# Graph attention on one core: from dense masked scores to a gathered list of edges

## The chip, the core and the metric

The kernel runs on one core of a Trainium2 chip. The metric is device time in microseconds (us). The kernel before took 4289.51 us, the median of 3 runs that lie between 4289.07 and 4289.96.

The engines are named as the profile names them: PE is TensorE (matrix products; PEld its weight loads), DVE is VectorE, ACT is ScalarE, POOL is GpSimd, and SP is SyncE, which here only starts transfers. SBUF is the on-chip memory of 128 partitions, PSUM holds the results of products, DRAM is the memory outside.

## The reference

There are 16 batches of 1024 nodes with 512 features, 8 heads of 64, and one 0/1 matrix `adj` of 1024 x 1024 for all batches. All is float32.

```python
q = (x @ Wq + bq).reshape(b, n, H, HD)          # k, v likewise
scores = einsum('bqhd,bkhd->bhqk', q, k) / sqrt(HD)
scores = scores + (1.0 - adj)[None, None, :, :] * -1e9
out = einsum('bhqk,bkhd->bqhd', softmax(scores, -1), v).reshape(b, n, d)
y = layernorm(x + out @ Wo + bo)
```

`adj` is sparse: entry (i, j) is 1 with probability 0.0039 times a weight that falls as one over the square root of i and of j. With the inputs given it has 4043 ones. The eight tiles of 128 rows have, counting a row without ones as one edge, 1404, 592, 446, 382, 368, 320, 301 and 290 edges, and the largest number in one row is 66, 10, 7, 9, 8, 6, 6 and 6. A row without ones gets the mean of all values, since its scores are all equally masked.

## The kernel before

All 1024 x 1024 scores of a head are computed, and a mask takes out those that aren't edges. `mask_setup` turns `adj` once into `maskT` (bf16, key by query: 0 or a large negative number). In `scores`, for a pair of heads, half of the queries (512) and a tile of 128 keys, PE makes two products with 64 rows (L325), DVE adds the mask while it takes the result out of PSUM (L329), ACT takes the exponential (L332), and POOL adds the result into a running sum over keys (L337, L339). `weigh` multiplies by the values (L347). `normalise` sums over partitions with a product with ones (L357), inverts (L359) and scales (L361).

While batch b runs, the pieces of `batch_work(b)` are put between: `finish` of batch b-1 (output projection L304, bias, residual, layer norm on DVE with a power on POOL, L301 to L316), the transposes of x for batch b+1 (L257) and its projections (`project_v` L266, `project_qk` L273). SP starts the loads of x and the stores of the result.

The tile framework orders the instructions of each engine when it builds the program, and puts in the waits; each engine then runs its list in order. So the order that a reader sees in the loops below isn't quite the order on an engine. Buffers are named by a tag and a number of copies (`bufs`); who asks for a copy waits until its last reader is done.

At the end a guard (`flag`) tests that the inputs are in the range that this method can do; if not, `tile_general` computes everything again in a general way.

Of the kernel before, what the change touches and what calls it, by code (L numbers as in the profile page):

```python
# [19 lines left out]
MASKED = -(2.0 ** 30)  # L20
LIMIT = (28.0 * 8.0) ** 2
# [101 lines left out]
def kernel(  # L123
# [25 lines left out]

    nc = tc.nc  # L150
# [4 lines left out]
    HALF = N // 2  # L155
    scale = 1.0 / HD ** 0.5
    assert N == 1024 and D == 512 and HD == 64

# [11 lines left out]

    with ExitStack() as main:
# [3 lines left out]
        psum = main.enter_context(tc.tile_pool(name="psum", bufs=1, space=bass.MemoryType.PSUM))  # L175

        def fill_psum(name):
            return psum.tile([P, HALF], F32, tag="fill", name=name, bufs=2)

        ones = one.tile([P, P], F32, name="ones")  # L180
        nc.gpsimd.memset(ones, 1.0)
        neg_half = one.tile([P, 1], F32, name="neg_half")
        nc.gpsimd.memset(neg_half, -0.5)

        pick = one.tile([P, 32], BF16, name="pick")
        nc.gpsimd.memset(pick, 0.0)
        nc.gpsimd.memset(pick[0:HD, 0:1], 1.0)
        nc.gpsimd.memset(pick[HD:P, 1:2], 1.0)
        gmax = one.tile([P, B * NPAIR], F32, name="gmax")
        maskT = one.tile([P, NT, N], BF16, name="maskT")  # L190
        nz_bc = one.tile([P, N], BF16, name="nz_bc")
        check = one.tile([P, NT], F32, name="check")

        XB, XT, V, QT, KT, OT, SQ = {}, {}, {}, {}, {}, {}, {}

        def load_x(b, t):

            if t < NT // 2:
                XB[b, t] = work.tile([P, 2, D], F32, tag="xb", name=f"xb_{b}_{t}", bufs=2)
                nc.sync.dma_start(XB[b, t], x[b, ds(t * 2 * P, 2 * P), :].rearrange("(j p) d -> p j d", p=P))  # L200
# [6 lines left out]
        nc.scalar.dma_start(bo_bc, bass.AP(tensor=bo.tensor, offset=bo.offset, ap=[[0, P], [1, D]]))  # L207

        def bias_setup():
# [7 lines left out]
            bvb = work.tile([P, NPAIR, P], F32, tag="y", name="bvb", bufs=2)  # L217
# [6 lines left out]
        def mask_setup(t):  # L224
            a = work.tile([P, N], F32, tag="prob", name=f"a_{t}", bufs=5)
            nc.sync.dma_start(a, adj[ds(t * P, P), :])
            j = work.tile([P, N], F32, tag="prob", name=f"a2_{t}", bufs=5)
# [14 lines left out]
            for k in range(NT):  # L242
                nc.tensor.transpose(pm[:, k // 4, ts(k % 4, P)], a[:, ts(k, P)], ident)  # L243
# [119 lines left out]
        def front_work(b):  # L363

            for t in range(NT):
                yield lambda t=t: project_v(b, t)
# [108 lines left out]
```

## Time and profile before

| what | value |
|---|---|
| median of 3 runs | 4289.51 us (4289.07 to 4289.96) |
| the profiled execution's own time | 4287.69 us |
| its span, first to last instruction | 4285.9 us |
| granted PE clock, mean | 0.992 |
| busy: PE, PEld, DVE, ACT, POOL | 4188.4, 1494.7, 2192.9, 1482.6, 2333.6 us |
| moved by DMA | 111.69 MB, mean 26 GB/s |

The span and the time of the same execution differ by 1.8 us. Busy time is the time in which at least one instruction of the engine ran; a product is shown longer than it holds PE, since products are pipelined. One float32 product is two rows of the trace on PE. A group's line names the source line, the engine, the operation, output and input, shapes, count, busy time and mean duration, and behind the second bar the idle time of that engine just before, with what ended it.

### The profile page before, as it was taken

The numbers are of one execution on the slowest core, as the hardware profiler recorded it, in microseconds if no ns is written. First come the engines' busy times: TensorE is split into PE (matmuls) and PEld (weight loads), VectorE is DVE, ScalarE is ACT, GpSimd is POOL, SyncE is SP. The second block draws the span as 40 slices with busy tenths as digits, with TensorE's granted clock in tenths as the row PEclk, the third lists the DMA queues.
The fourth block names the chain that finished last, engine by engine and source line by source line (L and its number), as shares of the span: only waits on it lengthen the run. The fifth ranks groups of instructions, "written<-read, shape, count | busy, mean of one in ns | idle before, by whom it ended". The sixth has DMA issues, their size and how long they took to land.

```text
span 4285.9 us, 35469 instructions
## 1 busy us (share of the span) xinstructions
PE 4188.4 (98%) x13660; PEld 1494.7 (35%) x13660; DVE 2192.9 (51%) x2200; ACT 1482.6 (35%) x1665; POOL 2333.6 (54%) x1163
## 2 busy tenths in 40 slices
PE   6999999999999999999999999999999999999987
PEld 3333333333333333333333333333333333333322
DVE  4345545454554544545455454545545445454565
ACT  1333333333333333333333333333333333333331
POOL 0355656555465555656555565554655556565575
PEclk8999999999999999999999999999999999999998
DMA  3000101010010100101000010100101001010001
GB/s 115 20 1 27 32 0 59 1 40 20 1 59 0 55 5 15 45 0 59 0 30 30 0 59 0 42 18 3 57 1 57 3 17 42 1 50 0 20 20 35
DMA packets 57882, 111.69 MB, mean 26 GB/s; under 512 B 5340, under 2 KB 5352, under 8 KB 57704
## 3 DMA queue, kind: packets, MB, share of 16 engines
q1 hardware_dynamic: 55424, 104.88, 7.7%
q10 hardware_dynamic: 2280, 4.46, 0.3%
q8 instruction: 109, 1.79, 0.2%
q14 instruction: 69, 0.57, 0.0%
HBM read 75.77 MB, written 33.55 MB: 26 GB/s over the span
## 4 chain that ended last, share of the span: by engine, by line
PE 92%; POOL 2%; DVE 2%; DMA 1%; issue 1%; ACT 0%; SPq 0%; POOLq 0%; DVEq 0%; ACTq 0%
PE sc L325 24%; PE av L347 21%; PE pv L266 11%; PE pq L273 11%; PE pk L273 11%; PE po L304 10%; PE den L357 3%; POOL acc L339 2%; PE pxT L257 2%; PE pg L294 1%; DMA y<-in_x_dram 1%; DVE rc L359 1%; DVE y L315 0%; DVE e L329 0%; DMA out_dram<-y 0%
## 5 line engine op out<-in xcount | busy, mean ns | idle before, releaser
L339 POOL TENSOR_TENSOR acc<-acc,e 128x1024 f32<-128x1024 f32 x768 | 1805.4, 2351 | 1113.1 <-ACT e L332 1081.8
L329 DVE TENSOR_TENSOR e<-sc,maskT 128x1024 f32<-128x1024 f32 x1024 | 1213.2, 1218 | 828.4 <-PE sc L325 828.0
L332 ACT ACTIVATE e<-e 128x1024 f32<-128x1024 f32 x1024 | 1082.5, 1057 | 1327.7 <-DVE e L329 1275.0
L325 PE MATMUL sc<-qT,kT 64*128 64x512 f32 x4096 | 1168.8, 622 | 12.8 <-DVE e L329 12.6
L347 PE MATMUL av<-e,v 128*64 128x512 f32 x4096 | 993.3, 606 | 0.0
L337 POOL TENSOR_TENSOR acc<-e,e 128x1024 f32<-128x1024 f32 x128 | 300.2, 2345 | 585.1 <-ACT e L332 585.0
L325 PEld LDWEIGHTS sc<-qT,kT 64*128 64x128 f32 x4096 | 385.0, 186 | 614.4 <-issue 505.7
L359 DVE RECIPROCAL rc<-den 128x512 f32<-128x512 f32 x128 | 429.5, 3355 | 145.8 <-PE den L357 145.8
L347 PEld LDWEIGHTS av<-e,v 128*64 128x64 f32 x4096 | 248.6, 136 | 683.4 <-issue 606.8
L304 PE MATMUL po<-wo,oT 128*128 128x512 f32 x1024 | 474.7, 607 | 3.0 <-DVE y L307 3.0
L266 PE MATMUL pv<-wv,xT 128*128 128x512 f32 x1024 | 472.7, 605 | 0.0
L273 PE MATMUL pq<-xT,wq 128*128 128x512 f32 x1024 | 472.5, 605 | 0.0
L273 PE MATMUL pk<-xT,wk 128*128 128x512 f32 x1024 | 472.2, 604 | 0.0
L304 PEld LDWEIGHTS po<-wo,oT 128*128 128x128 f32 x1024 | 185.0, 190 | 291.7 <-issue 271.9
L273 PEld LDWEIGHTS pq<-xT,wq 128*128 128x128 f32 x1024 | 184.4, 189 | 285.7 <-issue 285.7
L273 PEld LDWEIGHTS pk<-xT,wk 128*128 128x128 f32 x1024 | 184.6, 189 | 284.9 <-issue 284.9
L266 PEld LDWEIGHTS pv<-wv,xT 128*128 128x128 f32 x1024 | 184.8, 190 | 283.9 <-issue 248.2
L282 DVE SCALAR_TENSOR_TENSOR qT<-pq,bias_qk,nz_bc 128x512 f32<-128x512 f32 x128 | 96.1, 751 | 329.2 <-ACT sq L278 329.2
L295 DVE TENSOR_REDUCE gmax<-pg 128x1 f32<-128x512 f32 x64 | 44.3, 692 | 369.5 <-PE pg L294 369.5
L307 DVE TENSOR_TENSOR y<-po,y 128x512 f32<-128x512 f32 x128 | 88.1, 688 | 272.6 <-PE po L304 263.5
L278 ACT ACTIVATE sq<-pq,bias_qk 128x512 bf16<-128x512 f32 x128 | 87.9, 687 | 395.1 <-PE pq L273 395.1
L301 POOL TENSOR_TENSOR y<-y,bo_bc 128x512 f32<-128x512 f32 x128 | 163.0, 1273 | 108.9 <-PE pm L243 61.0
(65 smaller groups left out, 1201.1 us busy)
## 6 DMA issues: line engine op xcount, KB each, us to landing
xb<-in_x_dram SPq DMA_DIRECT2D x64, 512.0 KB, 3.7
y<-in_x_dram SPq DMA_DIRECT2D x128, 256.0 KB, 2.6
out_dram<-y SPq DMA_DIRECT2D x128, 256.0 KB, 2.1
a<-in_adj_dram SPq DMA_DIRECT2D x8, 512.0 KB, 4.5
wq<-in_L_gnn_Wq_dram ACTq DMA_DIRECT2D x1, 1024.0 KB, 9.0
wk<-in_L_gnn_Wk_dram ACTq DMA_DIRECT2D x1, 1024.0 KB
wv<-in_L_gnn_Wv_dram ACTq DMA_DIRECT2D x1, 1024.0 KB, 17.4
wo<-in_L_gnn_Wo_dram ACTq DMA_DIRECT2D x1, 1024.0 KB, 19.6
```

What stands on the lines that cost most here:

```text
L266: nc.tensor.matmul(p, XT[b][:, c, ts(t, P)], W["v"][:, c, :], start=(c == 0), stop=(c == NPAIR - 1))
L273: nc.tensor.matmul(p, W[name][:, c, ts(hp, P)], XT[b][:, c, ts(n, HALF)], start=(c == 0), stop=(c == NPAIR - 1))
L301: nc.gpsimd.tensor_tensor(y, y, bo_bc, op=OP.add)
L304: nc.tensor.matmul(p, OT[b, c, t // 4][:, ts(t % 4, P)], W["o"][:, c, :], start=(c == 0), stop=(c == NPAIR - 1))
L325: nc.tensor.matmul(sc[:, h, :], KT[b, hp][ts(h, HD), ts(kt, P)], QT[b, hp, n][ts(h, HD), :], start=True, stop=True)
L329: nc.vector.tensor_tensor(e, sc, maskT[:, kt, None, ts(n, HALF)].to_broadcast([P, 2, HALF]), op=OP.add)
L332: nc.scalar.activation(e, e, AF.Exp)
L337: nc.gpsimd.tensor_tensor(ACC[u], PR[b, hp, n, 0], e, op=OP.add)
L339: nc.gpsimd.tensor_tensor(ACC[u], ACC[u], e, op=OP.add)
L347: nc.tensor.matmul(AV[u][ts(h, HD), :], V[b, kt][:, ds(hp * P + h * HD, HD)], e[:, h, :], start=(kt == 0), stop=(kt == NT - 1),)
L357: nc.tensor.matmul(den[ts(h, HD), :], ones[:, 0:HD], acc[:, h, :], start=True, stop=True)
L359: nc.vector.reciprocal(rc, den)
```

## The change

The scores are computed for edges alone.

- **Edges (`edges`, once).** From `adj`, DVE takes the column numbers of the ones of each row out in order, 8 at a time (MAX, then a pass that sets those to zero): ten rounds for the first tile of 128 rows, two for the others. Each row gets a run of places in a list; blocks of 128 places are the unit of work. The eight tiles have 11, 6, 4, 4, 3, 3, 3 and 3 blocks (37 together). For each place the list holds the row of its key (`key_row`) and of its query (`query_row`); `sums` holds for each block a 128 x 128 0/1 matrix from places to queries.
- **Projections.** q, and k beside v, are computed per tile of 128 nodes with the nodes on partitions, and written to DRAM (`q_rows`, `kv_rows`; two copies each, by the batch's parity). The sums of squares for the guard are on ACT and DVE.
- **Per block (16 x 37 = 592).** `gather` starts two indirect transfers on POOL: 128 rows of k and v (4 KB each) and 128 rows of q (2 KB each). `scores` multiplies q and k on DVE and sums by head; ACT takes the exponential of 128 x 8 numbers. `weigh` multiplies the values by it on DVE. `add_up` sums over the edges of each query with two products with the 0/1 matrix. Masks, the large exponentials and POOL's running sums are gone.
- **Per tile of queries.** `normalise` divides, `transpose_o` transposes on PE for the output projection, `finish` is as it was.
- **Order.** `gather` runs 6 blocks ahead of `add_up`, `scores` 2 and `weigh` 1, as the loop is written. Each turn of the loop also takes one piece of the next batch's projections (24 per batch), or a `finish`.

The guard now also tests that each tile has no more edges than places, and no row more than 80 (first tile) or 16 ones.

The core of the diff (new text; what it replaces is named above):

```diff
-MASKED = -(2.0 ** 30)
-LIMIT = (28.0 * 8.0) ** 2
+LIMIT = 28.0 ** 2
+BLOCKS = (11, 6, 4, 4, 3, 3, 3, 3)
+DEGREE = (80, 16, 16, 16, 16, 16, 16, 16)
+KEYCODE = 2000.0
...
+        kv_rows = [dram.tile([N + 1, 2 * D], F32, name=f"kv_rows_{i}") for i in range(2)]
+        q_rows = [dram.tile([N, D], F32, name=f"q_rows_{i}") for i in range(2)]
...
+        def edges(t):
+            nb, J = BLOCKS[t], DEGREE[t]
+            a = work.tile([P, N], F32, tag="kvg", name=f"a_{t}", bufs=8)
             nc.sync.dma_start(a, adj[ds(t * P, P), :])
+            v = work.tile([P, N], F32, tag="kvg", name=f"codes_{t}", bufs=8)
+            nc.gpsimd.tensor_tensor(v, a, code, op=OP.mult)
...
+            for r in range(J // 8):
+                nc.vector.max(out=kl[:, ts(r, 8)], in_=v)
+                if r < J // 8 - 1:
+                    nc.vector.scalar_tensor_tensor(
+                        v, v, kl[:, r * 8 + 7:r * 8 + 8], v, op0=OP.is_lt, op1=OP.mult
+                    )
...
+            nc.vector.tensor_scalar(ge[:, 0:nb * P], span, kl[:, J:J + 1], None, op0=OP.is_ge)
+            nc.vector.scalar_tensor_tensor(of[:, 0:nb * P], span, end, ge[:, 0:nb * P], op0=OP.is_lt, op1=OP.mult)
...
+                for i in range(n):
+                    nc.tensor.matmul(g[:, i, :], of[:, ts(i0 + i, P)], kl, start=True, stop=True)
...
+        def norm(b, t, i, s):
...
+            nc.scalar.activation(sq, s, AF.Square)
+            nc.vector.tensor_reduce(
+                NRM[b][:, i, t, :], sq.rearrange("p (h d) -> p h d", d=HD), axis=AX.X, op=OP.add
+            )
+
+        def front_q(b, t):
+            p = project(b, t, "q")
+            q = work.tile([P, D], F32, tag="q", name=f"q_{b}_{t}", bufs=3)
+            nc.vector.scalar_tensor_tensor(q, p, scale, bq_bc, op0=OP.mult, op1=OP.add)
+            nc.sync.dma_start(q_rows[b % 2][ds(t * P, P), :], q)
+            norm(b, t, 0, q)
+
+        def front_k(b, t):
...
+            nc.vector.tensor_tensor(KV[b, t][:, 0:D], p, bk_bc, op=OP.add)
+            norm(b, t, 1, KV[b, t][:, 0:D])
+
+        def front_v(b, t):
...
+            nc.scalar.copy(kv[:, D:], p)
+            nc.sync.dma_start(kv_rows[b % 2][ds(t * P, P), :], kv)
...
+                nc.vector.tensor_tensor(VSUM[b], VSUM[b], kv[:, D:], op=OP.add)
...
+        def gather(n):
+            b, t, i = blocks[n]
+            g = first[t] + i
+            KG[n] = work.tile([P, 2 * D], F32, tag="kvg", name=f"kvg_{n}", bufs=8)
+            nc.gpsimd.indirect_dma_start(
+                out=KG[n], out_offset=None, in_=kv_rows[b % 2],
+                in_offset=bass.IndirectOffsetOnAxis(ap=key_row[:, g:g + 1], axis=0),
+            )
+            QG[n] = work.tile([P, D], F32, tag="qg", name=f"qg_{n}", bufs=8)
+            nc.gpsimd.indirect_dma_start(
+                out=QG[n], out_offset=None, in_=q_rows[b % 2],
+                in_offset=bass.IndirectOffsetOnAxis(ap=query_row[:, g:g + 1], axis=0),
+            )
+
+        def scores(n):
+            m = QG.pop(n)
+            nc.vector.tensor_tensor(m, m, KG[n][:, 0:D], op=OP.mult)
+            s = small.tile([P, HEADS], F32, tag="s", name=f"s_{n}", bufs=3)
+            nc.vector.tensor_reduce(s, m.rearrange("p (h d) -> p h d", d=HD), axis=AX.X, op=OP.add)
+
+            PV[n] = work.tile([P, D + HEADS], F32, tag="pv", name=f"pv_{n}", bufs=4)
+            nc.scalar.activation(PV[n][:, HD2:HD2 + HEADS], s, AF.Exp)
+
+        def weigh(n):
+            v, pv = KG.pop(n), PV[n]
+            for i in range(2):
+                nc.vector.tensor_tensor(
+                    pv[:, ds(i * (HD2 + HEADS), HD2)].rearrange("p (h d) -> p h d", d=HD),
+                    v[:, ds(D + i * HD2, HD2)].rearrange("p (h d) -> p h d", d=HD),
+                    pv[:, ds(HD2 + i * HEADS // 2, HEADS // 2), None].to_broadcast([P, HEADS // 2, HD]),
+                    op=OP.mult,
                 )
+
+        def add_up(n):
...
+            nc.tensor.matmul(SUM[b, t][:, 0, 0:HD2 + HEADS], m, pv[:, 0:HD2 + HEADS], **kw)
+            nc.tensor.matmul(SUM[b, t][:, 1, 0:HD2], m, pv[:, HD2 + HEADS:], **kw)
...
+        for n in range(total + 4):
...
+            if n + AHEAD < total:
+                gather(n + AHEAD)
...
+            if n + 2 < total:
+                scores(n + 2)
+            if n + 1 < total:
+                weigh(n + 1)
+            if n < total:
+                add_up(n)
...
+            old = bool(done) and done[0][0] < b
+            piece = None if old else next(fronts, None)
+            if piece:
+                piece()
+            elif done:
+                finish(*done.pop(0))
```

**What the change moves.** In the names below the first number of a block's tile is the block (204 is block 19 of batch 5, 222 the first of batch 6); other tiles have batch and tile.

VectorE in the middle of a batch, before (e is a tile of masked scores, sc the scores in PSUM):

```order
L329 TENSOR_TENSOR e_4_2_1_3_5427<-sc_4_2_1_3_5424,maskT_95 128x1024
L282 SCALAR_TENSOR_TENSOR qT_5_1_1_5443<-pq_5_1_1_5436,bias_qk_71,nz_bc_96 128x512
L329 TENSOR_TENSOR e_4_2_1_4_5448<-sc_4_2_1_4_5445,maskT_95 128x1024
L329 TENSOR_TENSOR e_4_2_1_5_5455<-sc_4_2_1_5_5452,maskT_95 128x1024
L329 TENSOR_TENSOR e_4_2_1_6_5475<-sc_4_2_1_6_5472,maskT_95 128x1024
L329 TENSOR_TENSOR e_4_2_1_7_5482<-sc_4_2_1_7_5479,maskT_95 128x1024
L295 TENSOR_REDUCE gmax_94<-pg_5_1_5498 128x1
L329 TENSOR_TENSOR e_4_3_0_0_5507<-sc_4_3_0_0_5504,maskT_95 128x1024
```

and now (block 200 to 208; `kvg` a block's gathered keys and values, `qg` its queries, which become the products, `pv` its weighted values, `nrm`, `kv_6_3` and `q_6_3` belong to the next batch's projections):

```order
L458 TENSOR_TENSOR qg_206_6568<-qg_206_6568,kvg_206_6566 128x512
L363 SCALAR_TENSOR_TENSOR q_6_3_6434<-pq_6_3_6429,bq_bc_104 128x512
L458 TENSOR_TENSOR qg_207_6589<-qg_207_6589,kvg_207_6587 128x512
L356 TENSOR_REDUCE nrm_6_6170<-sq_6_3_0_6437 128x8
L468 TENSOR_TENSOR pv_200_6517<-kvg_200_6395,pv_200_6517 128x256 x2
L460 TENSOR_REDUCE s_203_6592<-qg_203_6484 128x8
L370 TENSOR_TENSOR kv_6_3_6477<-pk_6_3_6472,bk_bc_105 128x512
L356 TENSOR_REDUCE nrm_6_6170<-sq_6_3_1_6479 128x8
L468 TENSOR_TENSOR pv_201_6541<-kvg_201_6416,pv_201_6541 128x256 x2
L460 TENSOR_REDUCE s_204_6625<-qg_204_6512 128x8
L458 TENSOR_TENSOR qg_208_6616<-qg_208_6616,kvg_208_6614 128x512
```

The products of block 208 (L458, the last row) stand six rows behind the weighing of block 200 (L468). There are 8 copies of `kvg`, so the gather of block 208 fills the copy that the weighing of block 200 gives back: what lies between these rows is the work that DVE has while that gather runs.

PE at about the same place, before (po is the output projection, sc and av scores and weighted values):

```order
L304 MATMUL po_7_2_9049<-wo_69,oT_7_0_0_8076 128x512
L304 MATMUL po_7_2_9049<-wo_69,oT_7_1_0_8360 128x512
L304 MATMUL po_7_2_9049<-wo_69,oT_7_2_0_8589 128x512
L304 MATMUL po_7_2_9049<-wo_69,oT_7_3_0_8831 128x512
L257 MATMUL pxT_9_1_0_9064<-ident_58,xb_9_1_8931 128x128 x4
L325 MATMUL sc_8_0_0_6_9078<-qT_8_0_0_8477,kT_8_0_8532 128x512
L257 MATMUL pxT_9_1_1_9070<-ident_58,xb_9_1_8931 128x128 x4
L325 MATMUL sc_8_0_0_6_9078<-qT_8_0_0_8477,kT_8_0_8532 128x512
L325 MATMUL sc_8_0_0_7_9085<-qT_8_0_0_8477,kT_8_0_8532 128x512 x2
L347 MATMUL av_8_0_0_9005<-e_8_0_0_4_9031,v_8_4_8367 64x512 x2
L347 MATMUL av_8_0_0_9005<-e_8_0_0_5_9038,v_8_5_8393 64x512 x2
```

and now (one piece of the next batch's projections, pv, pq or pk, after each block's two sums):

```order
L348 MATMUL pq_6_1_6274<-wq_63,xT_6_1_6227 128x512 x4
L481 MATMUL sum_5_0_6150<-pv_190_6248,sums_110 128x264
L482 MATMUL sum_5_0_6150<-pv_190_6248,sums_110 128x256
L339 MATMUL pxT_6_2_6298<-ident_58,x_6_2_6160 128x128 x4
L348 MATMUL pk_6_1_6307<-wk_65,xT_6_1_6227 128x512 x4
L481 MATMUL sum_5_0_6150<-pv_191_6268,sums_110 128x264
L482 MATMUL sum_5_0_6150<-pv_191_6268,sums_110 128x256
L348 MATMUL pv_6_1_6330<-wv_67,xT_6_1_6227 128x512 x4
L481 MATMUL sum_5_0_6150<-pv_192_6292,sums_110 128x264
L482 MATMUL sum_5_0_6150<-pv_192_6292,sums_110 128x256
L348 MATMUL pq_6_2_6352<-wq_63,xT_6_2_6303 128x512 x4
```

Each block now stands with one projection of four products, where such a projection stood with a pair of score products and value products before.

GpSimd around the end of a batch, before (acc is the running sum):

```order
L339 TENSOR_TENSOR acc_6_0_1_7004<-acc_6_0_1_7004,e_6_0_1_7_7142 128x1024
L301 TENSOR_TENSOR y_6_0_7897<-y_6_0_7897,bo_bc_72 128x512
L314 TENSOR_TENSOR rstd_7163<-rstd_7163,neg_half_88 128x1
L337 TENSOR_TENSOR acc_6_1_0_7180<-e_6_1_0_0_7171,e_6_1_0_1_7177 128x1024
L301 TENSOR_TENSOR y_6_1_7949<-y_6_1_7949,bo_bc_72 128x512
L339 TENSOR_TENSOR acc_6_1_0_7180<-acc_6_1_0_7180,e_6_1_0_2_7203 128x1024
L339 TENSOR_TENSOR acc_6_1_0_7180<-acc_6_1_0_7180,e_6_1_0_3_7210 128x1024
```

and now (the first gathers of batch 6; `rstd` and `y` belong to the layer norm of batch 5):

```order
L446 DMA kvg_222_7040<-kv_rows_0_115,key_row_111 128x1024
L446 DMA kvg_223_7060<-kv_rows_0_115,key_row_111 128x1024
L433 TENSOR_TENSOR rstd_6883<-rstd_6883,neg_half_88 128x1
L433 TENSOR_TENSOR rstd_6918<-rstd_6918,neg_half_88 128x1
L446 DMA kvg_224_7095<-kv_rows_0_115,key_row_111 128x1024
L416 TENSOR_TENSOR y_5_4_6850<-y_5_4_6850,bo_bc_72 128x512
L451 DMA qg_227_7168<-q_rows_0_117,query_row_112 128x512
L446 DMA kvg_225_7111<-kv_rows_0_115,key_row_111 128x1024
L433 TENSOR_TENSOR rstd_6946<-rstd_6946,neg_half_88 128x1
L451 DMA qg_228_7184<-q_rows_0_117,query_row_112 128x512
L416 TENSOR_TENSOR y_5_5_6951<-y_5_5_6951,bo_bc_72 128x512
L433 TENSOR_TENSOR rstd_6984<-rstd_6984,neg_half_88 128x1
```

The gathers take the place of the running sums, and the power for a tile's `rstd`, for which DVE waits, stands behind gathers that wait for copies of `kvg` which DVE gives back.

More of the change, by code (lines that the diff above doesn't have):

```diff
@@ L416 @@
[L416 to L431 removed]
+            edges(t)
```

387 lines of the change are left out of this document (208 added, 179 removed).

## The prediction

> **What bounds the kernel now.** I read the page's busy times first, then the chain of waits, then the costliest groups.
>
> ```profile
> span 4285.9 us, 35469 instructions
> PE 4188.4 (98%) x13660; PEld 1494.7 (35%) x13660; DVE 2192.9 (51%) x2200; ACT 1482.6 (35%) x1665; POOL 2333.6 (54%) x1163
> PE 92%; POOL 2%; DVE 2%; DMA 1%; issue 1%; ACT 0%; SPq 0%; POOLq 0%; DVEq 0%; ACTq 0%
> L339 POOL TENSOR_TENSOR acc<-acc,e 128x1024 f32<-128x1024 f32 x768 | 1805.4, 2351 | 1113.1 <-ACT e L332 1081.8
> L329 DVE TENSOR_TENSOR e<-sc,maskT 128x1024 f32<-128x1024 f32 x1024 | 1213.2, 1218 | 828.4 <-PE sc L325 828.0
> L325 PE MATMUL sc<-qT,kT 64*128 64x512 f32 x4096 | 1168.8, 622 | 12.8 <-DVE e L329 12.6
> L347 PE MATMUL av<-e,v 128*64 128x512 f32 x4096 | 993.3, 606 | 0.0
> L304 PE MATMUL po<-wo,oT 128*128 128x512 f32 x1024 | 474.7, 607 | 3.0 <-DVE y L307 3.0
> L266 PE MATMUL pv<-wv,xT 128*128 128x512 f32 x1024 | 472.7, 605 | 0.0
> ```
>
> PE is busy for 98% and carries 92% of the chain: the kernel is bound by products. Scores and value products take 1168.8 + 993.3 = 2162 us of PE; the four projections, each like the last two rows, about 1890 us. The first part goes, the second stays. So the question is which engine ends last once PE is relieved of half its work.
>
> **Prices.** A product's duration contains its pipeline, so I take distances between starts, from the order in time of PE and of DVE:
>
> ```profile
> 2003.30 3.70 PE L304 MATMUL po<-wo,oT 128*128 128x512 f32 x8
> 2006.84 0.60 PE L257 MATMUL pxT<-ident,xb 128*128 128x128 f32 x4
> 2007.37 1.12 PE L325 MATMUL sc<-qT,kT 64*128 64x512 f32 x2
> 14.53 1.21 DVE L229 TENSOR_REDUCE check<-a 128x1 f32<-128x1024 f32 x1
> 15.65 0.15 DVE L233 TENSOR_SCALAR mst<-mst 128x1 f32<-128x1 f32 x1
> L361 DVE TENSOR_TENSOR oT<-av,rc 128x512 f32<-128x512 f32 x128 | 88.4, 691 | 4.2
> L295 DVE TENSOR_REDUCE gmax<-pg 128x1 f32<-128x512 f32 x64 | 44.3, 692 | 369.5 <-PE pg L294 369.5
> L310 DVE BATCH_NORM_STATS2 stats<-y 128x6 f32<-128x512 f32 x128 | 88.9, 695 | 4.4
> L301 POOL TENSOR_TENSOR y<-y,bo_bc 128x512 f32<-128x512 f32 x128 | 163.0, 1273 | 108.9 <-PE pm L243 61.0 <-DMA y<-in_x_dram 29.2 <-DVE y L307 7.1
> L314 POOL TENSOR_TENSOR rstd<-rstd,neg_half 128x1 f32<-128x1 f32 x128 | 70.3, 549 | 136.6 <-DVE rstd L313 136.4
> ```
>
> PE: eight rows (four products of 512 columns) take 2006.84 - 2003.30 = 3.54 us, four transposes 0.53. DVE: a pass of 1.21 us frees the engine after 1.12, 0.09 earlier; so a pass over 512 costs 0.60 and, by the step from 691 to 1218 ns, one over 256 about 0.335.
>
> **What each block of 128 edges costs.** PE: 264 + 256 columns at 3.54/4/512 per column, 0.90 us. DVE: product 0.60, sum by head 0.60, two weighings 0.67, together 1.87. ACT's 128x8 exponential is short and off the path. POOL: two issues, whose price c no row shows. 592 blocks make 533 us on PE and 1107 on DVE.
>
> **What each of 128 tiles costs.** PE: four projections 14.16 and two groups of transposes 1.06. DVE: bias and scale 0.66 and 0.60, sums of squares 1.20, value sum 0.53, normalise about 0.87, finish about 1.82: 5.7. POOL: 1.27 + 0.55 = 1.82. Over the kernel PE has 533 + 1948 = 2481 us, DVE 1107 + 730 + about 70 for the edges (40 passes of 1.12 over 1024 columns, and short ones) = 1905, POOL 1184 c + 233.
>
> **The unknown c.** The nearest rows below and above: SP's issue of a transfer of this size, and POOL's own 1024-wide pass, 2.35 us.
>
> ```profile
> L300 SPq DMA_DIRECT2D y<-in_x_dram x128: 327/328/341, 59.8 to 4270.9; - x128
> xb<-in_x_dram SPq DMA_DIRECT2D x64, 512.0 KB, 3.7
> y<-in_x_dram SPq DMA_DIRECT2D x128, 256.0 KB, 2.6
> 0.00:20.00 20.00, 0.53 (x3) 0.56 (x4) 7.75 (x9) 1.28 (x1) 1.13 (x11) 1.00 0.92 331
> ```
>
> So c lies between 0.33 and 2.35. I take 1.3, near POOL's pass over 512 (1273 ns), since an issue has 128 indices to read, one per partition, and a POOL pass over 128 partitions costs 0.55 us even at one column; c is nearer to the lower end only if the indices are nearly free. The Trainium skill, DMA: Bandwidth & Descriptors, in its section on specifications, gives about 1 us to the first byte on GpSimd's path against 0.6 from SP; with c = 1.0 instead of 1.3 the sum below would be about 175 us less. No row of this case shows it.
>
> **The transfers.** 592 x 0.75 MiB gathered (466 MB), 101 MB written to the row tables, 101 MB for x twice and the result, some 8 more: 675 MB. In the first 20 us 331 GB/s flowed at a busy share of 0.92, so full engines move 360: 1876 us. That is no bound by itself but under two thirds of the span that follows.
>
> **One batch.** The order list has 24 blocks that each stand with one projection: PE 0.90 + 3.54 + 0.53/3 + some transposes of outputs = 4.65, DVE 8.6/3 = 2.9, POOL 2c = 2.6. PE sets the pace if the buffers let it. A copy of `kvg` is 8 blocks long in use; by the order list about 6.3 of them lie between a block's products and its weighing, so the other 1.7 paces must hold the round trip: issue 1.3, landing 3.7, and a query gather ahead of it in queue and engines, 1.3 + 0.7: 7.0, so 4.1 per block. 4.65 holds: 24 x 4.65 = 112 us.
>
> The other 13 blocks have the finishes. PE: 44. DVE: 24 + 8 x 1.82 + 5 x 0.87 = 43. POOL: 26 c + 8 x 1.82 = 48. Three near equals that wait for each other: `rstd` stands behind gathers, and DVE's last pass of a tile waits for it, where before POOL had only sums in hand. I add per tile a gather's issue, the power and a hand-over, 1.3 + 0.55 + 0.25, 8 x 2.1 = 17: 65 us. One batch is 177.
>
> **The start.** The first pass over `adj` began at 12.3 us:
>
> ```profile
> 12.26 1.23 DVE L228 SCALAR_TENSOR_TENSOR a<-a 128x1024 f32<-128x1024 f32 x1 [12.26 <-DMA a<-in_adj_dram]
> 40.00:60.00 20.00, 8.94 (x38) 6.47 (x38) 19.55 (x34) 0.28 (x1) 0.00 (x0) 0.64 0.27 89
> 4260.00:4286.00 26.00, 8.04 (x18) 3.03 (x18) 12.20 (x30) 0.00 (x0) 7.17 (x8) 0.78 0.22 77
> ```
>
> Then POOL's product (2.35), 19 passes of 1.12 for the first tile (21), its expansion (12): 48. Each of the 8 tiles then has three projections (10.6) with about 4 us of DVE passes that PE waits for: 117. With the first gather, 5, this makes 170. Before, the start had the same projections in a closed row on PE, so these aren't hidden in either.
>
> **The sum.** 170 + 15 x 177 = 2825. The last batch has no projections: POOL 74 c + 8 x 1.82 = 111, with waits 130. The end, after the last block, is like the last 26 us of before without its weighing: 22. Together 2977, and 2 us lie around the span (4287.69 against 4285.9; the three runs have 4289.51, 2 more): **2980 us**.
>
> In the last two rows the granted clock is 0.64 and 0.78 where PE is busy for under half of the time. In the 13 blocks PE is at 44 of 65; even at 0.8 its 44 become 55, still inside the 65. So the clock changes nothing unless PE stalls in the 24 as well.
>
> **Its own range.** With c = 0.33 the 13 blocks are set by PE and DVE, 46 us, the last batch by DVE, 95: 170 + 15 x 158 + 95 + 24 = 2660. With c = 2.35 POOL sets everything: 24 blocks 113 to 120, the 13 blocks (61 + 15) and 8 x 3.15 = 101, the last batch 190: 170 + 15 x 221 + 190 + 24 = 3700.
>
> **Rivals.**
>
> *GpSimd and VectorE lock each other out.* For it:
>
> ```profile
> L315 DVE TENSOR_SCALAR y<-y,mv,rstd x128: 537/547/2579, 399.9 to 4278.0; 128x512 f32<-128x512 f32 x128
> ```
>
> A DVE pass with median 547 ns once lasted 2579, longer by about one POOL pass (2351): the two exclude each other for whole instructions. DVE's block work now reads two SBUF operands for 1.27 of 1.87 us, so an issue on POOL may have to wait for the pass in hand, some 0.4 us each: c = 1.7. The 24 blocks stay PE's (82 us of POOL); the rest become 26 x 1.7 + 15 + 20 = 79, the last batch 155: 170 + 15 x 191 + 155 + 24 = 3214. Against it: whether an issue takes that port no row shows. The Trainium skill, SBUF — State Buffer, in the section on two separate sides, says that with DVE in a two-port mode GpSimd can't write descriptors, and the transfer looks blocked, while two SBUF inputs shut out only GpSimd work that reads SBUF. By that rule only the last pass of each `finish` blocks for certain (128 x 0.55 = 70 us), and the time would be some 3050.
>
> *The round trip decides everywhere.* If the gathers' rows, scattered and shared with writes, flow at 220 GB/s, between the 142 of a lone load (512 KB in 3.7 us) and the 360 of full engines, one batch's 42 MB need 191 us, and PE waits in the 24 blocks too: 170 + 15 x 200 + 130 + 24 = 3320. For it: a gather is bound to its buffer's release; against it: rows of 2 and 4 KB are as long as those of x, which flowed at 331.
>
> *The waits don't show.* Issue is cheap and short stalls are absorbed by the buffers: 2660 to 2800, about 2750.
>
> *Slower than before.* POOL's issue goes through the 128 indices one after the other and costs more than any row here. Once 48 c exceeds 112, everything follows POOL: 170 + 15 x (48 c + 1.25 x 26 c + 20) + 74 c + 50 is about 1282 c + 520, which passes 4288 at c = 2.94; at c = 3.3 it gives 4750. For it, only that no row prices an issue; against it, 3.3 us is beyond any POOL row.
>
> *It doesn't do what it says.* If the guard found too many edges, the general path would run behind everything. With these inputs the largest tile has 1404 edges for 1408 places and the largest row 66 of 80, so I leave this at nothing.
>
> **How the numbers follow.** Chances: the forecast 0.40, lock 0.18, round trip 0.16, no waits 0.17, slower 0.09. The likeliest gives 2980. For the range I leave out the slower case and the far end of c = 2.35: 2670 to 3620. A measurement of this kernel tells 0.2% from no change; the cases that end below 4281 have 0.905, above 4298 0.09, between them 0.005.
>
> **What would show it.** PE busy about 2480 us, near 85% of the span, DVE between 1900 and 2300, as its passes overlap in the rows; `kvg` and `qg` issues some 1.3 us apart on POOL where they queue. In the first 24 blocks of a batch PE without gaps and the clock at 1.0; in the 13 around a batch's end, DVE waiting for POOL's `rstd` and for gathers. It is wrong if POOL's issues stand without gaps in the whole span (c above 2.3), or if DVE waits for gathers while PE is idle in the middle of a batch (round trip).

## The result and the profile after

The changed kernel took 2923.82 us, the median of 4 runs (2917.59 to 2934.78), beside 4289.29 us for the kernel before on the same chip (4 runs, 4287.69 to 4289.96): a ratio of 0.682, with a 95% interval from 0.680 to 0.684. The forecast was 2980. The profiled execution took 2934.78 us, 11 above the median.

These are the lines of the changed kernel's page that answer to those of before: the span, the busy times, the bytes, the chain by engine, and four groups.

```profile
span 2933.0 us, 27152 instructions
PE 2578.4 (88%) x7659; PEld 1377.0 (47%) x7659; DVE 2013.0 (69%) x4375; ACT 488.1 (17%) x1300; POOL 1488.4 (51%) x1462
...
HBM read 541.86 MB, written 134.25 MB: 231 GB/s over the span
...
DMA 27%; DVE 25%; issue 21%; POOL 15%; PE 12%; ACT 1%; POOLq 0%; DVEq 0%; SPq 0%; ACTq 0%
...
L446 POOL DMA_INDIRECT kvg<-kv_rows,key_row x592 | 599.0, 1012 | 907.7 <-DVE pv L468 800.5
L458 DVE TENSOR_TENSOR qg<-qg,kvg 128x512 f32<-128x512 f32 x592 | 407.6, 693 | 545.3 <-DMA kvg<-kv_rows,key_row 540.7
...
L348 PE MATMUL pv<-wv,xT 128*128 128x512 f32 x1024 | 481.1, 614 | 42.8 <-DVE q L363 42.8
...
L434 DVE TENSOR_SCALAR y<-y,mv,rstd 128x512 f32<-128x512 f32 x128 | 73.9, 577 | 162.6 <-POOL rstd L433 162.6
```

PE has the most work still (88%), but it no longer carries the chain: 12%, where it was 92%. The chain goes round between gathers, DVE and POOL. Read the idle columns as a loop: POOL's gathers of keys and values wait 800.5 us for DVE's weighing (L468), which gives a copy of `kvg` back; DVE's products (L458) wait 540.7 us for those same gathers. PE waits little for any one of them (42.8 us in the largest row here); its losses are short stalls behind those of DVE.

A batch by its two parts: the 24 blocks with projections (first row) and the 13 around the batch's end (second row), from the windows view of the changed kernel. The columns are the stretch, its length, busy time of PE, PEld, DVE, ACT and POOL with instructions in brackets, granted PE clock, DMA share, GB/s.

```profile
1062.40:1186.00 123.60, 116.30 (x337) 60.62 (x338) 79.06 (x164) 20.89 (x56) 58.60 (x57) 0.97 0.73 244
1186.00:1239.50 53.50, 44.79 (x136) 24.11 (x134) 42.70 (x106) 7.21 (x22) 34.42 (x35) 0.90 0.70 230
```

By the order in time of PE, the first part takes 118 to 124 us and the second 52 to 58 us in the 14 whole batches. The period comes from a copy that runs once in the projections of each batch, as its line's view lists it, and from the second of these copies:

```profile
L388 ACT COPY mean<-pm x16: 575/575/576, 186.6 to 2769.7; 1x512 f32<-1x512 f32 x16
```

```profile
311.98 0.57 ACT L388 COPY mean<-pm 1x512 f32<-1x512 f32 x1 [5.53 <-PE pm L386]
```

The first copy belongs to the projections of batch 0, in the start. The second stands at the end of the 24 blocks of batch 0, and each later one at the end of the 24 blocks of the next batch. So 14 whole periods lie between the second and the last: (2769.7 - 312.0) / 14 = 175.5 us, where 177 was forecast. The span falls into four parts:

| part | forecast, us | measured, us | difference |
|---|---|---|---|
| the start, up to the first copy | 170 - 5 = 165 | 186.6 | +22 |
| first gather and 24 blocks of batch 0 | 5 + 112 = 117 | 125.4 | +8 |
| 14 periods | 14 x 177 = 2478 | 2457.7 | -20 |
| 13 blocks, last batch and end | 65 + 130 + 22 = 217 | 163.3 | -54 |

The copy runs 3 us behind the last projection in the start and 9 to 10 us behind it later, so some 7 us of the second part belong to the fourth. Together the span is 44 us below the sum of 2977. The total is near because errors of both signs met in it, and that is luck; the experiments take them apart.

**The price of an issue**, the unknown of the prediction. POOL where gathers queue, in order of time, and then the view of the gathers' line, with min/median/max of the instruction and of the time to landing:

```profile
1187.15 0.94 POOL L446 DMA_INDIRECT kvg<-kv_rows,key_row  x1 [6.28 <-DVE pv L468]
1188.40 0.95 POOL L451 DMA_INDIRECT qg<-q_rows,query_row  x1 [0.30 <-issue]
1189.65 0.95 POOL L451 DMA_INDIRECT qg<-q_rows,query_row  x1 [0.30 <-DVE nrm L356]
1190.91 0.94 POOL L446 DMA_INDIRECT kvg<-kv_rows,key_row  x1 [0.30 <-DVE pv L468]
```

```profile
L446 POOL DMA_INDIRECT kvg<-kv_rows,key_row x592: 932/942/2726, 192.1 to 2890.9; - x198
...
DMA to landing us min/median/max: 3.9/5.4/9.5
```

Starts are 1.25 us apart: 0.94 of work and 0.30 between. The same price for keys with values (4 KB rows) and queries (2 KB rows): it doesn't go by bytes. Landing, counted from the start of the issue, takes 5.4 us in the median.

**How a stall travels.** DVE and then PE of the changed kernel in order of time, in the middle of the 24 blocks:

```profile
1118.52 0.68 DVE L383 TENSOR_TENSOR vsum<-vsum,kv 128x512 f32<-128x512 f32 x1
...
1120.59 0.68 DVE L460 TENSOR_REDUCE s<-qg 128x8 f32<-128x512 f32 x1
1122.85 0.69 DVE L458 TENSOR_TENSOR qg<-qg,kvg 128x512 f32<-128x512 f32 x1 [1.57 <-DMA kvg<-kv_rows,key_row]
1123.46 0.68 DVE L363 SCALAR_TENSOR_TENSOR q<-pq,bq_bc 128x512 f32<-128x512 f32 x1
```

```profile
1116.38 3.60 PE L348 MATMUL pk<-wk,xT 128*128 128x512 f32 x8
...
1121.46 0.59 PE L482 MATMUL sum<-pv,sums 128*128 128x256 f32 x2
1124.19 3.70 PE L348 MATMUL pv<-wv,xT 128*128 128x512 f32 x8 [2.14 <-DVE q L363]
...
1153.56 5.40 PE L348 MATMUL pv<-wv,xT 128*128 128x512 f32 x8 [1.92 <-DVE q L363]
```

DVE stands at a product for a gather. Behind it in DVE's list is the pass that takes `pq` out of PSUM (L363), and PE can't begin `pv` before that: 2.14 us. Between such stalls PE goes at 4.31 to 4.75 us per block. Some stalls cost twice: the eight rows after 1153.56 took 5.40 us instead of 3.60, and the granted clock (the third number from the end) was 0.69 there:

```profile
1153.50:1159.00 5.50, 5.44 (x9) 2.41 (x10) 3.36 (x8) 2.42 (x7) 0.41 (x1) 0.69 0.41 141
```

### The profile page after: what moved, and what is told of

The parts are those of the page before. It is cut to its first block, busy times and chain, and to the rows that moved or that the text cites. A ratio compares the mean times of both kernels' runs of the same rounds, so it can differ in the third digit from the quotient of the medians.

```text
span 2933.0 us, 27152 instructions
## 1 busy us (share of the span) xinstructions
PE 2578.4 (88%) x7659; PEld 1377.0 (47%) x7659; DVE 2013.0 (69%) x4375; ACT 488.1 (17%) x1300; POOL 1488.4 (51%) x1462
## 4 chain that ended last, share of the span: by engine, by line
DMA 27%; DVE 25%; issue 21%; POOL 15%; PE 12%; ACT 1%; POOLq 0%; DVEq 0%; SPq 0%; ACTq 0%
DMA kvg<-kv_rows,key_row 22%; POOL qg L451 8%; DVE s L460 5%; DVE pv L468 5%; DVE qg L458 4%; POOL kvg L446 4%; PE po L424 3%; POOL rstd L433 2%; DVE kv L370 2%; DVE nrm L356 2%; DVE stats L429 2%; PE pq L348 2%; PE pv L348 2%; DVE y L426 2%; PE pk L348 2%
## 5 line engine op out<-in xcount | busy, mean ns | idle before, releaser
L446 POOL DMA_INDIRECT kvg<-kv_rows,key_row x592 | 599.0, 1012 | 907.7 <-DVE pv L468 800.5
L458 DVE TENSOR_TENSOR qg<-qg,kvg 128x512 f32<-128x512 f32 x592 | 407.6, 693 | 545.3 <-DMA kvg<-kv_rows,key_row 540.7
L451 POOL DMA_INDIRECT qg<-q_rows,query_row x592 | 615.7, 1040 | 259.6 <-issue 105.7
L348 PE MATMUL pv<-wv,xT 128*128 128x512 f32 x1024 | 481.1, 614 | 42.8 <-DVE q L363 42.8
L348 PE MATMUL pq<-wq,xT 128*128 128x512 f32 x1024 | 473.1, 605 | 34.9 <-ACT xT L341 34.9
L468 DVE TENSOR_TENSOR pv<-kvg,pv 128x256 f32<-128x256 f32 x1184 | 487.7, 436 | 0.0
L348 PE MATMUL pk<-wk,xT 128*128 128x512 f32 x1024 | 460.8, 593 | 2.0 <-DVE kv L370 2.0
L460 DVE TENSOR_REDUCE s<-qg 128x8 f32<-128x512 f32 x592 | 400.3, 676 | 0.0
L481 PE MATMUL sum<-pv,sums 128*128 128x264 f32 x1184 | 371.6, 396 | 13.8 <-DVE pv L468 9.9
L482 PE MATMUL sum<-pv,sums 128*128 128x256 f32 x1184 | 363.2, 389 | 4.7 <-DVE pv L468 4.4
L481 PEld LDWEIGHTS sum<-pv,sums 128*128 128x128 f32 x1184 | 218.5, 195 | 202.1 <-issue 171.9
L482 PEld LDWEIGHTS sum<-pv,sums 128*128 128x128 f32 x1184 | 229.9, 195 | 49.0 <-DVE pv L468 8.0
```

Source lines behind the costliest of these rows:

```text
L348: nc.tensor.matmul(p, XT[b, t][:, ts(c, P)], W[name][:, c, :], start=(c == 0), stop=(c == NPAIR - 1))
L446: nc.gpsimd.indirect_dma_start(out=KG[n], out_offset=None, in_=kv_rows[b % 2], in_offset=bass.IndirectOffsetOnAxis(ap=key_row[:, g:g + 1], ...
L451: nc.gpsimd.indirect_dma_start(out=QG[n], out_offset=None, in_=q_rows[b % 2], in_offset=bass.IndirectOffsetOnAxis(ap=query_row[:, g:g + 1] ...
L458: nc.vector.tensor_tensor(m, m, KG[n][:, 0:D], op=OP.mult)
L460: nc.vector.tensor_reduce(s, m.rearrange("p (h d) -> p h d", d=HD), axis=AX.X, op=OP.add)
L468: nc.vector.tensor_tensor(pv[:, ds(i * (HD2 + HEADS), HD2)].rearrange("p (h d) -> p h d", d=HD), v[:, ds(D + i * HD2, HD2)].rearrange("p ( ...
```

## The experiments

The theories. **A**: the changed kernel is held by the round trip of a gather through the 8 copies of `kvg`, because DVE's list puts the products of block n shortly behind the weighing of block n-8. **B**: it is the bytes, or the rate at which scattered rows flow. **C**: it is PE's work alone. Later **R**: in the 13 blocks it is the hand-over DVE - POOL - DVE for `rstd`. And **Y**: it is POOL, standing at the addition to `y` until a load lands. Every run was compared with the kernel before on its own chip; the ratios in brackets carry 95% intervals.

### A longer way for the gathers (m2)

```diff
-            QG[n] = work.tile([P, D], F32, tag="qg", name=f"qg_{n}", bufs=8)
+            QG[n] = work.tile([P, D], F32, tag="qg", name=f"qg_{n}", bufs=6)
...
-            m = QG.pop(n)
-            nc.vector.tensor_tensor(m, m, KG[n][:, 0:D], op=OP.mult)
+            m = work.tile([P, D], F32, tag="prod", name=f"prod_{n}", bufs=2)
+            nc.vector.tensor_tensor(m, QG.pop(n), KG[n][:, 0:D], op=OP.mult)
```

> The products of queries and keys go into a tile of their own with 2 copies (and the gathered queries have 6 copies instead of 8, so that it fits in SBUF). This holds DVE's products at most 4 blocks ahead of the weighing, where the changed kernel has 6 to 7; at least 9.6 us of DVE passes then lie between a block's weighing and the first reading of the block 8 later, where there were 2.1 to 5.3. Theory A (the round trip through the 8 copies, too short by the order on DVE, is what stalls PE): DVE's wait for gathered keys falls from 541 us to under 100, the 24 blocks with projections from 124 us to about 114, the other 13 from 48 to 53 down to about 45, so 15 x (10 to 18) less: 2650 to 2780 us. Rival B (the transfers themselves, their rate and their landing, set the pace): the wait only moves, 2900 to 2940.

Measured: 2805.17 us (0.653 to 0.655 of before), 119 less than the changed kernel. Windows of m2, the same two parts of a batch:

```profile
1007.80:1120.80 113.00, 111.57 (x338) 59.73 (x338) 89.04 (x179) 22.78 (x59) 60.75 (x61) 1.00 0.83 276
1120.80:1171.70 50.90, 42.45 (x136) 24.02 (x134) 35.94 (x81) 6.60 (x19) 27.40 (x29) 0.90 0.62 197
```

DVE's wait for gathered keys and values, from the view of the products' line (us, times); it was 540.7 us in the changed kernel:

```profile
  DMA kvg<-kv_rows,key_row: 3.9, 1
```

The direction is A's, and so is the wait, which was to fall below 100; the time is 25 us above A's range. In the 24 blocks the stall is gone: PE is busy for 111.57 of 113.00 us, at clock 1.00. DVE's products, which may now be at most four blocks ahead of the weighing, leave the work of four blocks in DVE's list for a round trip, where one or two were left when the products ran six or seven ahead. But the 13 blocks only fell from 53.5 to 50.9 and not to A's 45, although DVE waits for gathers no more, so what sets them is something else, or something more.

### Fewer bytes (half_rows), and both (m2_half)

```diff
-        kv_rows = [dram.tile([N + 1, 2 * D], F32, name=f"kv_rows_{i}") for i in range(2)]
+        kv_rows = [dram.tile([N + 1, D], F32, name=f"kv_rows_{i}") for i in range(2)]
...
-                out=KG[n], out_offset=None, in_=kv_rows[b % 2],
+                out=KG[n][:, 0:D], out_offset=None, in_=kv_rows[b % 2],
...
-                    v[:, ds(D + i * HD2, HD2)].rearrange("p (h d) -> p h d", d=HD),
+                    v[:, ds(i * HD2, HD2)].rearrange("p (h d) -> p h d", d=HD),
```

> Leaves out the values: the row table holds keys only, 2 KB instead of 4 KB per row, and keys are weighed in the place of values. Gathered bytes fall from 466 to 310 MB, written ones from 101 to 67, the issues stay 1184. The order on DVE gets tighter by it: 1.4 to 2.5 us of passes between the weighing and the products 8 blocks later in most blocks, and the products are 6 to 7 blocks ahead. Theory A: the landing falls from 5.4 to about 4.3 us, but only about 1.4 paces hold it: (1.25 + 4.3 + 1.25) / 1.4 = 4.9 us per block, so no gain, 2880 to 3050. Rival B: a quarter to a third fewer bytes, 100 to 250 us less: 2670 to 2820.

> Both edits together: product tile of its own, and keys in the place of values with half the row. Theory A: the gathers are covered already, so like the product tile alone within 40 us (2650 to 2780). Rival B: 150 us or more below the product tile alone.

Measured: half_rows 3048.53 us (0.708 to 0.711), m2_half 2730.92 (0.635 to 0.638). The waits view of half_rows (engine, line, what it waited for; us, times, longest) and its windows, then those of m2_half:

```profile
DVE qg L458 <- DMA kvg<-kv_rows,key_row: 652.5, 359, 4.7
```

```profile
1104.50:1230.00 125.50, 115.00 (x338) 59.86 (x338) 81.09 (x165) 20.79 (x56) 56.11 (x55) 0.99 0.55 168
1230.00:1287.80 57.80, 44.21 (x136) 24.58 (x134) 42.13 (x99) 7.20 (x22) 34.77 (x36) 0.88 0.53 158
```

```profile
1000.40:1113.40 113.00, 111.29 (x338) 59.89 (x338) 88.72 (x177) 23.00 (x59) 60.14 (x60) 1.00 0.62 194
1113.40:1161.20 47.80, 42.15 (x135) 24.08 (x134) 37.49 (x86) 6.59 (x19) 30.54 (x32) 0.93 0.55 169
```

With a third less gathered, at 168 instead of 244 GB/s, the changed kernel became 125 us slower, and DVE waits more for gathers (652.5 against 540.7). Bytes are not what holds the 24 blocks: B falls for them. That it is slower agrees with A, since in this kernel's list the products stand still closer behind the weighing that frees their copy; that this is the whole of the 125 us wasn't tested. With the longer way, half the bytes take 74 us more off, nearly all of it outside the 24 blocks (113.0 in both): less than B's 150, more than A's 40. There the transfers do count: POOL's wait for `y` fell from 180.9 to 101.4 us and DVE's for `rstd` from 221.1 to 144.8.

### Less work on PE (short_proj, m2_short)

```diff
-            for c in range(NPAIR):
-                nc.tensor.matmul(p, XT[b, t][:, ts(c, P)], W[name][:, c, :], start=(c == 0), stop=(c == NPAIR - 1))
+            for c in range(NPAIR - 1):
+                nc.tensor.matmul(p, XT[b, t][:, ts(c, P)], W[name][:, c, :], start=(c == 0), stop=(c == NPAIR - 2))
```

> Leaves out a quarter of each projection of q, k and v (3 of 4 products over the features). PE has 340 us less work, 0.885 per projection. Rival C (PE's stream alone sets the pace of the 24 blocks): all of it, 2560 to 2620. Theory A (the round trip of issue 1.25, landing 5.4 and one more issue 1.25 over 1.7 paces is 4.65 us per block, the same as PE's): the gathers hold the pace, 50 to 170 us less, 2750 to 2870. Rival B as A.

> Both edits: products of q and gathered keys go to a tile of their own (as in m2), and each of the projections of q, k and v leaves out its last of four products (as in short_proj, so the output is not that of the reference). PE has some 340 us less than in m2. Theory A (in short_proj half of that was lost to the round trip through the kvg copies): with the longer way for the gathers nearly all of it shows, the 24 blocks of a batch fall from 113-118 us to 92-98, time 2805 - 15 x 21 - 20 = 2430 to 2520. Theory B (transfers: at 243 GB/s in m2 the engines are near what scattered rows let through): 280 GB/s would be needed, so the time stays above 2600.

Measured: short_proj 2750.17 us (0.639 to 0.643), m2_short 2506.95 (0.583 to 0.586). The first 24 blocks of each, short_proj and then m2_short:

```profile
1156.00:1261.20 105.20, 94.62 (x290) 50.83 (x290) 76.82 (x156) 20.08 (x54) 57.97 (x56) 0.98 0.81 274
```

```profile
1052.30:1147.70 95.40, 92.53 (x290) 51.88 (x290) 84.22 (x174) 21.88 (x59) 59.71 (x60) 0.98 0.93 322
```

340 us less on PE bought 174 us in the changed kernel and 298 in m2. So in the changed kernel PE and the round trip were at the same height: taking from the one alone shows the other. C falls, A stands. And the rows flowed at 322 GB/s in m2_short, so 244 in the changed kernel was no limit of theirs.

### The hand-over for rstd (no_pow, m2_no_pow)

```diff
             nc.vector.tensor_scalar(rstd, mv[:, 1:2], EPS, None, op0=OP.add)
-            nc.gpsimd.tensor_tensor(rstd, rstd, neg_half, op=OP.pow)
             nc.vector.tensor_scalar(y, y, mv[:, 0:1], rstd, op0=OP.subtract, op1=OP.mult)
```

> The changed kernel without the power on POOL: variance plus epsilon is used in place of its inverse root, so the output is not that of the reference. In m2 this took 192 us off. Theory A (in the changed kernel the round trip of the gathers sets the 13 blocks too, and takes up what rstd gives back): 2850 to 2924. Rival (the two waits add up, each on its own): 2730 to 2800, with the 13 blocks near 42 us.

> m2 without the power on POOL: variance plus epsilon is used in place of its inverse root, so the output is not that of the reference. Theory R (DVE's wait for rstd behind gathers, 221 us in m2, sets the 13 blocks around a batch's end): most of it goes, 2600 to 2680. Theory Y (POOL itself stands in those blocks, waiting 181 us for the loads of y ahead of gathers in its queue; rstd is late because of that): 2730 to 2790, and y's loads are waited for as long as before.

Measured: no_pow 2892.55 us (0.672 to 0.676), m2_no_pow 2612.74 (0.608 to 0.610). The 13 blocks of no_pow and its wait for gathers, then both parts of a batch of m2_no_pow and its wait for `y`:

```profile
1172.40:1223.60 51.20, 42.48 (x134) 23.17 (x134) 41.71 (x106) 7.20 (x22) 28.67 (x27) 0.93 0.69 223
```

```profile
DVE qg L457 <- DMA kvg<-kv_rows,key_row: 634.8, 401, 6.8
```

```profile
954.40:1067.20 112.80, 111.35 (x337) 59.95 (x338) 88.85 (x180) 23.00 (x59) 59.82 (x61) 1.00 0.83 285
1067.20:1109.30 42.10, 40.11 (x135) 22.56 (x134) 38.77 (x85) 6.59 (x19) 23.22 (x21) 1.00 0.66 211
```

```profile
POOL y L416 <- DMA y<-in_x_dram: 214.5, 59, 8.6
```

Here is what the 13 blocks wait for. Each of the two waits covers the other:

| taken away | us | less than the changed kernel | the 13 blocks of one batch |
|---|---|---|---|
| nothing | 2923.82 | | 53.5 |
| the power (no_pow) | 2892.55 | 31 | 51.2 |
| the short way of the gathers (m2) | 2805.17 | 119 | 50.9 |
| both (m2_no_pow) | 2612.74 | 311 | 42.1 |

31 and 119 make 150; both together give 311, and the 13 blocks fall to 42.1 us, where PE is busy for 40.11. In no_pow DVE's wait for gathers grew to 634.8 us (from 540.7) and took up what `rstd` gave back: A there, R in m2. Y falls for m2: its 192 us went although POOL waited longer for `y` (214.5 us, 180.9 in m2).

### Moving y, and one power for two tiles (late_y, m2_late_y, m2_ly_pair)

In `late_y` and `m2_late_y` a helper loads `y` for the next three tiles to be finished, and adds the bias for the next two, in place of a load and an addition at a tile's first block. `m2_ly_pair` also shares the power:

```diff
-            nc.gpsimd.tensor_tensor(y, y, bo_bc, op=OP.add)
+        def prepare(done):
+            for d in done[:3]:
+                if d not in Y:
+                    load_y(*d)
+            for d in done[:2]:
+                if d not in ADDED:
+                    ADDED.add(d)
+                    nc.gpsimd.tensor_tensor(Y[d], Y[d], bo_bc, op=OP.add)
...
+            nc.vector.tensor_scalar(rstd[:, t % 2:t % 2 + 1], mv[:, 1:2], EPS, None, op0=OP.add)
+            late.append((t, y, mv))
+            if t % 2 == 1:
+                nc.gpsimd.tensor_tensor(rstd, rstd, neg_half, op=OP.pow)
+                for i, (t, y, mv) in enumerate(late[1:]):
+                    nc.vector.tensor_scalar(y, y, mv[:, 0:1], rstd[:, i:i + 1], op0=OP.subtract, op1=OP.mult)
+                    nc.sync.dma_start(out[b, ds(t * P, P), :], y)
```

> The changed kernel with only the loads of y and their POOL addition moved as in m2_late_y. The output is that of the reference. POOL waits 50 us for y in the changed kernel. Theory A (the round trip through the kvg copies sets the changed kernel in all blocks): 2890 to 2925, a small gain at most. Theory Y: y's place in POOL's queue costs as much here as in m2: 2780 to 2860.

> m2 with the loads of y and their POOL addition of the bias moved: not at the first block of a tile, but when the tile is within three (load) or two (addition) of its finish, so that POOL does not stand at an addition whose load waits for a free copy. The output is that of the reference. Theory Y (POOL's stand at y, 181 us in m2, delays gathers and rstd in the 13 blocks): 2650 to 2740, the 13 blocks fall from 48-53 us to 40-46. Theory R (rstd and the hand-overs between PE, DVE and POOL in finish set those blocks): within 25 of m2, 2780 to 2820.

> m2_late_y with one power on POOL for two tiles of a batch instead of one for each: DVE meets POOL's queue 64 times instead of 128. The output is that of the reference. Theory R (the hand-over DVE - POOL - DVE behind gathers sets the 13 blocks; without it m2 came to 2613): half of the 160 us between m2_late_y (2775) and that go, 2680 to 2720, and DVE's wait for rstd halves from 220 us to 90-130. Rival: the wait per hand-over doubles, because the first tile of a pair now holds its y copy longer and POOL's queue is as long: within 25 of m2_late_y, 2750 to 2800.

Measured: late_y 2938.72 us (0.684 to 0.686), m2_late_y 2774.77 (0.646 to 0.648), m2_ly_pair 2719.18 (0.633 to 0.636). Waits of m2_late_y, then waits and windows of m2_ly_pair:

```profile
DVE y L444 <- POOL rstd L443: 219.9, 122, 7.0
...
POOL y L427 <- DMA y<-in_x_dram: 140.4, 43, 6.3
```

```profile
DVE y L449 <- POOL rstd L447: 133.6, 56, 6.4
```

```profile
989.40:1103.10 113.70, 111.58 (x338) 59.94 (x338) 87.60 (x177) 22.87 (x59) 60.21 (x60) 1.00 0.81 275
1103.10:1147.80 44.70, 41.29 (x135) 23.77 (x133) 36.51 (x82) 6.59 (x19) 27.66 (x27) 0.96 0.71 227
```

Moving `y` in the changed kernel gained nothing: it came out 15 us above it, 14 above A's range and far from Y's. In m2 the move gained 30, between the two expectations: it took only 40 of POOL's 181 us of waiting for `y` away, so it is no clean test of Y. Halving the number of hand-overs then gained 56 more, which is the small end of R's range (2680 to 2720), and POOL's wait for `y` fell by another 38 us beside it; the wait for `rstd` is 133.6 us, a little above R's 90 to 130, since each wait that is left got longer (133.6 / 56 = 2.4 us instead of 219.9 / 122 = 1.8). At 2719 us m2_ly_pair is 7% below the changed kernel.

## Why the prediction came out as it did

The time came near the forecast, but by the prediction's own signs its mechanism failed in the 24 blocks. PE was to run there without gaps at clock 1.0; it was busy for 116.30 of 123.60 us at 0.97. And "if DVE waits for gathers while PE is idle in the middle of a batch" was its sign of being wrong: the rows at 1122.85 and 1124.19 above show just that.

**What it had right.** The bound before, and the relief: a batch's 24 blocks at "24 x 4.65 = 112 us" is what PE takes there when nothing stalls it (113.00 and 112.80 us in m2 and m2_no_pow). The price of an issue, c = 1.3, against 1.25 measured. The Trainium skill, DMA: Bandwidth & Descriptors, in its section on specifications, gives about 1 us to the first byte on this path; the time for which the instruction holds POOL is another quantity, but comes near it (0.94), and what a queue of gathers pays is 1.25, the instruction and the 0.30 between. DVE at 2013 us lies in its 1900 to 2300.

**The step that failed in the 24 blocks** is the round trip and its room: "the other 1.7 paces must hold the round trip: issue 1.3, landing 3.7, and a query gather ahead of it in queue and engines, 1.3 + 0.7: 7.0, so 4.1 per block. 4.65 holds". That the copies of `kvg` and the order of DVE's list close a loop was right. One turn of it, from the weighing of block 198 to the gather of block 206, which takes its copy (the products of block 206 are the row at 1122.85 above):

```profile
1116.03 0.75 DVE L468 TENSOR_TENSOR pv<-kvg,pv 128x256 f32<-128x256 f32 x2
```

```profile
1117.05 0.94 POOL L446 DMA_INDIRECT kvg<-kv_rows,key_row  x1 [1.11 <-DVE pv L468]
```

The weighing ends at 1116.78, the gather starts 0.27 us later, and the products start at 1122.85: a trip of 6.07 us. (Over the 344 turns of the 14 whole batches in which DVE stood for such a gather, the median trip is 5.8 us.) Two of its terms were mis-sized, in opposite ways. Landing takes 5.4 us in the median and not the 3.7 of a plain load; both are counted from the issue, so the issue is in them. And nothing stood ahead: POOL was waiting for this weighing, as for 322 of the 592 gathers of keys and values. So the trip is shorter than the 7.0 us priced, and the room is what failed. At 4.65 us a pace, 1.7 paces would be 7.9 us. But the passes of DVE's list aren't spread over PE's paces: after this weighing it has passes until 1121.27, and then it stands 1.57 us. The expectation for m2 put this room at 2.1 to 5.3 us of passes in the changed kernel and at 9.6 or more in m2, and the wait followed it, from 540.7 to 3.9 us. That 1.25 + 5.4 + 1.25 us over 1.7 paces, in the expectation for short_proj, gives PE's 4.65 is chance, since in such a turn the issues it adds aren't on the way. That taking work from PE alone is half lost to this loop is what short_proj and m2_short show.

**The clock.** "The clock changes nothing unless PE stalls in the 24 as well" names the condition, and the condition came true. PE was busy for 2578.4 us where 2481 were priced, at a mean clock of 0.951; in m2_no_pow, with the same products and a clock of 0.985, it was busy for 2475.4. Some 100 us of PE time are thus low clock, of which the part inside stalls costs nothing.

**The step that failed in the 13 blocks**, the other way, is "I add per tile a gather's issue, the power and a hand-over ... 8 x 2.1 = 17: 65 us". Two terms were mis-sized. POOL's 48 us were not the base: 35 POOL instructions ran there and not 26 + 16 = 42, since the gathers run ahead into the 24 blocks, and POOL was busy for 34.4 of 53.5 us. The base was PE and DVE, priced at 44 and 43; without both waits the stretch took 42.1. And the waits came to 53.5 - 42.1 = 11 us, not 17; part of them is DVE's wait for gathers, which the 17 don't hold and which runs side by side with the wait for `rstd`. 15 x 11 us too many here and 15 x 9 too few in the 24 blocks nearly cancel: this, and not an exact sum, brought a batch within 1.5 us of its forecast.

**The last batch and the end** are the largest error, 33 us: 98.7 + 20.2 us instead of 130 + 22. From PE's first sum of the last batch to its last, by the windows view:

```profile
2814.10:2912.80 98.70, 75.93 (x231) 44.41 (x230) 87.85 (x200) 11.08 (x41) 67.95 (x69) 0.86 0.78 259
```

The forecast counted 74 issues and 16 other instructions on POOL, 111 us with 19 for waits. Only 69 POOL instructions ran in this stretch, for 67.95 us, since gathers had run ahead here too. DVE, busy for 87.85 us, was the fuller engine.

**The start** was some 20 us too short, in the list of edges. DVE's groups, then rows in order of time of POOL, DVE and PE:

```profile
L273 DVE MAX8 kl<-codes 128x8 f32<-128x1024 f32 x24 | 28.9, 1218 | 7.9 <-POOL codes L263 7.8
L275 DVE SCALAR_TENSOR_TENSOR codes<-codes,kl 128x1024 f32<-128x1024 f32 x16 | 26.0, 1633 | 0.1
```

```profile
21.65 5.65 POOL L263 TENSOR_TENSOR codes<-a,code 128x1024 f32<-128x1024 f32 x2 [9.51 <-DMA a<-in_adj_dram]
```

```profile
22.31 2.78 DVE L275 SCALAR_TENSOR_TENSOR codes<-codes,kl 128x1024 f32<-128x1024 f32 x1
```

```profile
57.03 4.99 PE L304 MATMUL pe<-kl,of 128*128 128x82 f32 x22 [23.57 <-DVE kl L273]
...
65.89 3.70 PE L348 MATMUL pq<-wq,xT 128*128 128x512 f32 x8 [0.68 <-ACT xT L341]
```

The expansion of the first tile (L304) began at 57.0 us, where 12.3 + 2.35 + 21 = 36 was forecast, and the first projection at 65.9 instead of 48. The 21 us for the first tile's 19 passes counted them as if they ran alone. Before 60 us 25 passes of both kinds had run, those of other tiles among them, for 37 us in all, and three of the selections took 2.78 to 3.38 us in place of 1.3.

**The rivals.** The lock between POOL and DVE hardly shows on the issues: the median is 0.942 us where the shortest is 0.932, with DVE busy 69% of the time. All 1184 issues together took (599.0 + 615.7) - 592 x (0.942 + 0.953) = 93 us more than their medians; what lengthened those few, and how much of it reached the span, wasn't tested. The round trip deciding everywhere, at 220 GB/s and 3320 us, was right that DVE waits for gathers in the 24 blocks too, and wrong about the rate: with 322 GB/s in m2_short, 231 was an outcome. "The waits don't show", 2660 to 2800, is where the kernel went once waits were taken out (2719 in m2_ly_pair; 2613, below it, in m2_no_pow). An issue beyond 2.94 us didn't occur.

## What to carry to other kernels

A gather into a ring of buffers has a budget: the work that the consumer's list holds between the last use of a copy and the first use of what refills it. Compare it with the trip from release to landing, price that with a gather and not with a plain load, and look at the order of the list, not at the number of buffers. Here a second tile for the products, with no more memory, moved the budget from 2.1 to 5.3 us to at least 9.6 against a trip of some 6, and the wait went. Two waits that run side by side each look nearly worthless when taken away alone (2.3 and 2.6 us of the 13 blocks here, 11.4 together), so try the pair before giving either up.

## What was not expected of the hardware

- PE's clock fell after stalls of about 2 us: eight rows of 512 columns took 5.40 us after one of 1.92 us, yet 3.70 after one of 2.14. In the changed kernel's trace behind the start, the granted clock went to 0.5 after 2 of 23 stalls of 1 to 2 us, 7 of 13 of 2 to 2.5 us, 5 of 6 of 2.5 to 3 us and all 28 of 3 to 6 us (the ends of products are modelled, so these lengths are rough). The Trainium skill, TensorE: Matmul & The Clock Gate, in its part on the clock gate, puts the step down behind an idle window of about 3.4 us that runs freely; the uneven outcome fits a window that doesn't start with the stall, but that so short a stall sufficed doesn't fit the length, and no run here settles it.
- Reading half of the key and value rows made the changed kernel 125 us slower. It also moved the products closer behind the weighing in DVE's list; whether that is the whole reason wasn't tested.
- DVE's 1024-wide selection pass (L275) took 1.26 to 1.29 us in 13 of 16 cases. The other three, 2.78, 3.35 and 3.38 us, are the ones that began while POOL's product over 1024 columns (L263) was running; the MAX passes (L273) that began then took no longer than the others, 1.2 us.
